# An attention stage on one core: rows of two heads' halves in turn, three strip transfers, masked maxima from a constant, and the subtraction products split over both sets of a step

## The chip, the core and the metric

The kernel runs on one core of a Trainium2 chip. TensorE (PE) multiplies, VectorE (DVE) and ScalarE (ACT) read its results out of PSUM, GpSimd (POOL) works on SBUF alone, and SyncE (SP) issues most transfers. The metric is device time in microseconds (us) of one execution, as the median of several runs; lower is better.

## The reference, cut to what matters

The model is four layers on `x` of 4 batches x 1024 positions x 256 channels: latent attention, a gated feed-forward scan, a delta-rule layer, and the feed-forward scan again. The change lies in the attention alone, whose core is

```python
c_kv = x @ W_dkv.T
q = (x @ W_dq.T @ W_uq.T).reshape(B, T, nh, hs)
q_lat = einsum('bqhd,hdl->bhql', q, k_eff)
attn = einsum('bhql,bkl->bhqk', q_lat, c_kv) / sqrt(hs)   # 16 heads of 16
attn = where(causal, attn, -inf)
attn = softmax(attn, axis=-1)
y = einsum('bhql,hld->bqhd', attn @ c_kv, v_eff)
```

The softmax needs, for every query, its greatest unmasked score before the exponentials are taken.

## The kernel before

The 64 (batch, head) pairs are worked in 16 **units** of four heads (`units`, L77). For each unit three buffers of 128 partitions x 1024 positions hold its strips: `kh` and `kl` (the keys as a high part and a rest) and `q`. Head j of the unit has partitions 32j to 32j+31; in them the 16 key rows stand twice, and beside them in `q` the queries' high part (first 16 rows) and rest (second 16). One product over 32 rows with `kh` and one with `kl` thus give a score of full precision, and the four heads' products lie on four different strips of 32 rows of TensorE's array.

`quad(i, s)` (L366) is one **step**: ten steps make a unit (`STEPS`, L54), and each step does one piece of up to 512 columns for all four heads of *two* units at once:

- for unit i+1 (`first`, in the code `one` is True) the scores with queries on partitions, in two passes (`kh`, `kl`), from which VectorE takes **maxima** (`finish`, L421 to L432). Steps 0 to 2 and 7 to 9 hold the diagonal and use a fused add-mask-and-maximum (L424); steps 3 to 6 are a plain maximum (L430) into `m0`. The diagonal pieces of the second half of the queries start their maximum from that `m0` column.
- for unit i (`second`) the scores with keys on partitions, in three passes: `kh`, `kl`, and `gr` with the weights `minus`, which subtracts each query's greatest score. ScalarE takes the exponentials (L419) into `p`. On diagonal steps a matmul of `identb` with `mb` puts the mask into the bank first (`masks`, L386).

Each of these eight results of a step has a PSUM bank of its own out of a pool of seven (`pss`, L74), which also serves every other small product. A step is issued as two **sets** with the value products of two steps ago between them (L445 to L461; `values`, L480): in the first set the heads 2 and 3 of unit i and 0 and 1 of unit i+1, in the second set the others. All four `gr` products of unit i stand in the first set, on all four strips, so the banks of unit i's heads 0 and 1 are opened there: six banks in the first set, two in the second.

`greatest(i, half)` (L464) turns the 128 x 16 maxima of a half by TensorE into `ps_m`, splits them into a high part and a rest (ACT L470, DVE L471), and sends them through DRAM (`md`) into the `gr` rows. The first half of unit i+1 is turned behind step 4 of `quad(i)`, the second half of unit i behind step 0 of `quad(i)`, straight after that step's second set (L587, put first among the step's places).

`feature` (L272) makes the rows of `kall` and `qall` of one batch (two row blocks `mc`, two column halves `n`) and writes them to DRAM; `heads(i, j)` (L313) fetches unit i's strips from there, six transfers of 16 rows for each head, 24 to a unit, all from SP's queue, which keeps its order. For unit 0 the strips are made directly (`first_feature`, L296).

The order on every engine is written out by hand (`manual_schedule`, L520): the loop from L556 calls `quad`, `values`, and the extra work that was put into `places` of each step. Before unit 0's exponentials comes `quad(-1)`, ten steps with unit 0's maxima alone; the other work of batch 0 (features, `vals`, strips of unit 1) is dealt out over its steps 3 to 9 (L570), the strips of unit 1 behind all features.

## Time and profile before

| | |
|---|---|
| median of 3 runs | 1326.14 us (1324.3 to 1327.25) |
| the profiled execution's own time | 1326.79 us |
| its span (first to last instruction) | 1325.1 us |
| mean granted TensorE clock | 0.98 |
| attention stage | from 0 to about 650 us of the span |
| `quad(-1)` | about 20 to 52 us |
| steps with maxima and exponentials together | about 52 to 622 us, 150 of them |

Engine times are busy times. A busy PE isn't a PE at its peak: its rows overlap, and a row's end is modelled, so the place where a stage begins and the next one begins is the better measure. "PEld" is the loading of weights. In the timeline view a row is start, duration, engine, line, operation, result and operands, shape and count, and in brackets the idle time before it with what ended it. The waits view has who waited for whom, then the total, the number of waits and the longest. `ps_s<-q,kh` with 32 rows is a product for the exponentials or the maxima: the compiler's names put the moving operand first, so `q,kh` is unit i's (exponentials) and `kh,q` unit i+1's (maxima).

### The profile page before, as it was taken

Reading aid. Unit: us, or ns where it says so; the run is one execution under the profiler, and the core shown is the slowest. Engines: PE = TensorE matmul, PEld = TensorE weight load, DVE = VectorE, ACT = ScalarE, POOL = GpSimd, SP = SyncE. Lnnn points to the kernel's source line nnn. Section 1 sums busy time; section 2 is a strip of 40 time slices with the busy share of each in tenths; the row PEclk is TensorE's granted clock in tenths of the full one; section 3 lists DMA queues with packets and bytes.
Section 4 is the critical chain, followed back from the end, with each engine's and each line's share of the span. In section 5 each row is a group of like instructions: output and inputs, shape, how many; then the busy total and the mean of one; then the engine's idle time right before and its main releaser. Section 6 shows DMA issues by size and latency. Waiting matters only on the chain. (4 is left out here: it accounts for less than half of the span.)

```text
span 1325.1 us, 36572 instructions
## 1 busy us (share of the span) xinstructions
PE 1247.8 (94%) x14596; PEld 776.4 (59%) x14596; DVE 840.2 (63%) x2440; ACT 697.5 (53%) x1626; POOL 423.3 (32%) x681
## 2 busy tenths in 40 slices
PE   7899899999999999999999999898988999899997
PEld 3454455545555555555444766665655677677886
DVE  6786678787787877886122454468879767533333
ACT  3266566666666666666623456445655544334432
POOL 1040002323033110122100245346888745535220
PEclk9799899999999999999999999999999999999999
DMA  3812621334221422220300223215364532333210
GB/s 96 208 51 70 186 67 48 79 96 146 68 53 41 133 79 59 67 51 4 112 17 0 78 75 90 80 26 166 99 169 112 139 90 75 111 102 85 64 64 32
DMA packets 118649, 112.23 MB, mean 85 GB/s; under 512 B 46672, under 2 KB 103504, under 8 KB 118480
## 3 DMA queue, kind: packets, MB, share of 16 engines
q1 hardware_dynamic: 95200, 100.39, 27.6%
q10 hardware_dynamic: 23280, 9.51, 2.7%
q8 instruction: 115, 1.88, 0.6%
q14 instruction: 54, 0.44, 0.1%
HBM read 65.22 MB, written 44.63 MB: 83 GB/s over the span
## 5 line engine op out<-in xcount | busy, mean ns | idle before, releaser
L419 ACT ACTIVATE p<-ps_s 128x512 f32<-128x512 f32 (+1 forms) x640 | 319.3, 554 | 199.7 <-PE ps_s L410 196.5
L410 PE MATMUL ps_s<-kh,q 32*128 32x512 f32 (+3 forms) x768 | 189.3, 425 | 8.8 <-DMA q<-qall 5.1
L430 DVE TENSOR_REDUCE m<-ps_s 128x1 f32<-128x512 f32 x256 | 163.0, 681 | 34.9 <-PE ps_s L410 34.5
L410 PE MATMUL ps_s<-q,kh 32*128 32x512 f32 (+3 forms) x768 | 163.2, 424 | 0.4
L488 PE MATMUL ps_y<-p,vb 128*32 128x512 f32 (+3 forms) x1536 | 158.3, 500 | 1.1 <-ACT ys L494 1.0
L410 PE MATMUL ps_s<-kl,q 32*128 32x512 f32 (+3 forms) x768 | 151.7, 357 | 0.0
L424 DVE CUSTOM_DVE_ANT_0 junk<-ps_s,mask,m 128x512 bf16<-128x512 f32 (+3 forms) x256 | 126.4, 545 | 38.3 <-PE ps_s L410 37.6
L424 DVE CUSTOM_DVE_ANT_0 junk<-ps_s,mask 128x512 bf16<-128x512 f32 (+3 forms) x256 | 112.3, 486 | 48.9 <-PE ps_s L410 48.5
L410 PE MATMUL ps_s<-q,kl 32*128 32x512 f32 (+3 forms) x768 | 131.2, 359 | 0.0
L410 PEld LDWEIGHTS ps_s<-q,kh 32*128 32x128 f32 x768 | 73.9, 184 | 77.1 <-issue 45.8
L512 POOL TENSOR_TENSOR xa<-xa,yt 128x256 f32<-128x256 f32 x32 | 23.4, 731 | 275.7 <-DVE yt L508 275.7
L410 PEld LDWEIGHTS ps_s<-kh,q 32*128 32x128 f32 x768 | 89.1, 185 | 28.1 <-ACT p L419 9.8
L410 PE MATMUL ps_s<-gr,minus 32*128 32x512 f32 (+3 forms) x768 | 98.2, 365 | 6.1 <-DMA gr<-md 4.9
L391 PEld LDWEIGHTS <-identb 128*128 128x128 bf16 x512 | 34.4, 98 | 88.2 <-issue 85.8
L410 PEld LDWEIGHTS ps_s<-kl,q 32*128 32x128 f32 x768 | 81.4, 188 | 0.0
L205 POOL TENSOR_SCALAR rs<-mv 128x2 f32<-128x2 f32 x24 | 5.5, 230 | 236.6 <-DVE mv L204 236.6
L410 PEld LDWEIGHTS ps_s<-gr,minus 32*128 32x128 f32 x768 | 67.6, 187 | 19.7 <-DMA gr<-md 5.3
L1120 DVE SCALAR_TENSOR_TENSOR gate<-gate 128x256 f32<-128x256 f32 (+1 forms) x56 | 29.4, 524 | 76.3 <-ACT gate L1099 76.1
L1080 PE MATMUL ps_gate<-xnT,ffn_wi 128*128 128x256 f32 (+1 forms) x224 | 66.0, 418 | 3.5 <-DVE hh L1193 3.3
L1198 POOL TENSOR_TENSOR x<-x,hh 128x256 f32<-128x256 f32 x56 | 44.0, 800 | 75.0 <-ACT hh L1197 54.2
L772 PE MATMUL ps_kqv<-wa,h 128*128 128x512 f32 x128 | 65.5, 634 | 2.4 <-ACT h L762 2.3
L410 PEld LDWEIGHTS ps_s<-q,kl 32*128 32x128 f32 x768 | 67.2, 186 | 0.0
(228 smaller groups left out, 2626.5 us busy)
## 6 DMA issues: line engine op xcount, KB each, us to landing
x<-x SPq DMA_DIRECT2D x30, 512.0 KB
kh<-kall SPq DMA_DIRECT2D x120, 64.0 KB
kl<-kall SPq DMA_DIRECT2D x120, 64.0 KB
q<-qall SPq DMA_DIRECT2D x120, 64.0 KB
kall<-hl SPq DMA_DIRECT2D x14, 512.0 KB
qall<-hl SPq DMA_DIRECT2D x12, 512.0 KB
kept<-gs ACTq DMA_DIRECT2D x32, 192.0 KB
gl<-kept SPq DMA_DIRECT2D x32, 192.0 KB
```

Of the source, the lines that this page charges most:

```text
L205: nc.gpsimd.tensor_scalar(rs, mv[:, :, 1], EPS, None, ALU.add)
L391: nc.tensor.matmul(ps[:, ds(at, P)], identb, mb, start=x == 0 and (False, j) not in begun, stop=True, skip_group_check=True,)
L410: nc.tensor.matmul(ps[:, ds(at, n)], a, m, start=x == 0 and (one, j) not in begun, stop=last, skip_group_check=True,)
L419: nc.scalar.activation(p[:, j, :width], ps[:, :width], AF.Exp)
L424: nc.vector.tensor_tensor_reduce(out=junk[:, :n], in0=ps[:, ds(at, n)], in1=mask[:, 512 - n :], scale=1.0, scalar=-3e38 if qt < 4 else fir ...
L430: nc.vector.tensor_reduce(first.m0[:, j, qt - 4 : qt - 3], ps[:, ds(at, n)], AX.X, ALU.max)
L488: nc.tensor.matmul(u.y[ds(32 * j, 32), q0:], vb[u.b % 2][:, kt, ds((4 * u.g + j) * VS, 32)], u.p[s][:, j, ds(at, n)], start=kt == 0, stop= ...
L512: nc.gpsimd.tensor_tensor(xs, xs, yt.rearrange("p n j d -> p n (j d)"), ALU.add)
L772: nc.tensor.matmul(dst, hT(c, kc), wt[:, kc, :], start=kc == 0, stop=kc == KC - 1)
L1080: nc.tensor.matmul(ps, f["w" + "fic"[j]][:, kc, ds(m * P, P)], k.xnT[:, kc, t, ds(at, width)], start=kc == 0, stop=t == 0 and kc == KC - 1,)
L1120: nc.vector.scalar_tensor_tensor(acts[1], acts[1], 1.0, acts[2], ALU.add, ALU.mult)
L1198: nc.gpsimd.tensor_tensor(x[:, b, :], x[:, b, :], h, ALU.add)
```

## The change

Four edits, in the diff's order.

1. **Rows in turn.** The 32 rows of a head stand as row 0 high, row 0 rest, row 1 high, ... in place of 16 high and then 16 rest. `wk0`, `wq0` and the column that picks the rest (`second_half`, now `odd`, one sum over every other column of the identity) follow it.
2. **Three transfers.** `heads(i, x)` fetches `kh`, `kl` and `q` of a unit by one transfer each of 128 rows, the key rows read twice by a broadcast. For unit 1 the order in `quad(-1)` is laid out anew: the first row block's features in steps 2 and 3, unit 1's strips at step 4 ahead of the other features, which go to steps 4 to 7, `vals` in steps 7 to 9.
3. **Maxima from a constant.** Every fused maximum starts at -3e38. In its place `greatest(i, 1)` begins with one VectorE maximum of `m` and `m0`, 128 x 16, ahead of the turn.
4. **Each set with its own `gr` products.** Both sets run three passes, the third with two products in place of four and none. Each set opens four banks.

```diff
-            nc.gpsimd.memset(second_half, 1.0)
...
+            nc.vector.tensor_reduce(odd, k.ident[:, ds(1, P // 2, step=2)], AX.X, ALU.add)
...
-            rs = ds(64 * u.g + HS * j, HS)
-            k_, q_ = bt.kall.bitcast(F32), bt.qall.bitcast(F32)
-            for a in range(2):
-                to = ds(32 * j + HS * a, HS)
-                for dst, src in ((u.kh, k_[0, rs]), (u.kl, k_[1, rs]), (u.q, q_[a, rs])):
-                    nc.sync.dma_start(out=dst.bitcast(F32)[to, :], in_=src)
+            rs = ds(64 * u.g, 64)
+            if x < 2:
+                dst, src = (u.kh, u.kl)[x], bt.kall.bitcast(F32)[x, rs].unsqueeze(1).broadcast_to([64, 2, T])
+            else:
+                dst, src = u.q, bt.qall.bitcast(F32)[:, rs].rearrange("a r t -> r a t")
+            nc.sync.dma_start(out=dst.bitcast(F32), in_=src)
...
-                            scalar=-3e38 if qt < 4 else first.m0[:, j, qt - 4 : qt - 3],
+                            scalar=-3e38,
...
-                masks((2, 3))
-                for turn_ in range(2):
-                    for one, j in ((False, 2), (True, 0), (False, 3), (True, 1)):
-                        product(one, j, turn_, one and turn_ == 1)
-                for j in (2, 3):
-                    product(False, j, 2, True)
-                for j in (0, 1):
-                    product(False, j, 2, False)
...
+                    masks([j for one, j in order if not one])
+                    for turn_ in range(3):
+                        for one, j in order:
+                            if not (one and turn_ == 2):
+                                product(one, j, turn_, turn_ == (1 if one else 2))
+                    for one, j in order:
+                        finish(one, j)
...
             u = units[i]
+            if half:
+                nc.vector.tensor_tensor(u.m[:, 1], u.m[:, 1], u.m0, ALU.max)
             ps = pss.tile([16, P], F32, tag="s", name="ps_m")
             nc.tensor.transpose(ps, u.m[:, half].rearrange("p j q -> p (j q)"), k.ident)
...
+                        first[2 + n if mc == 0 else 4 + 2 * n + y].append(
+                            lambda mc=mc, n=n, name=name, wt=wt, of=of: feature(0, mc, n, name, wt, of, True)
+                        )
+            for y in range(3):
+                first[4].insert(y, lambda y=y: heads(1, y))
```

More of the change, by code (lines that the diff above doesn't have):

```diff
@@ L123, in attention @@
         minus = wp.tile([P, P], F32R, name="minus")
-        second_half = wp.tile([P, 1], F32, name="second_half")
+        odd = wp.tile([P, 1], F32, name="odd")
         wk0, wq0 = (wp.tile([P, P], F32, name=n) for n in ("wk0", "wq0"))
@@ L133, in first_rows @@
             )
-            for j in range(4):
-                d = second_half[ds(32 * j, 32), :]
-                nc.gpsimd.affine_select(
-                    out=d, in_=d, compare_op=ALU.is_ge, fill=0.0, base=-HS, pattern=[[0, 1]],
-                    channel_multiplier=1,
-                )
             for g in gr:
                 nc.vector.memset(g.bitcast(F32), 0.0)
+            nc.vector.tensor_reduce(odd, k.ident[:, ds(1, P // 2, step=2)], AX.X, ALU.add)
         VS = HS + 1
@@ L173, in attention @@
             nc.scalar.activation(
-                wq0.rearrange("p (j a r) -> p j a r", j=4, a=2)[:, :, a],
+                wq0.rearrange("p (j r a) -> p j r a", j=4, a=2)[:, :, :, a],
                 ps[:, 0, 0:64].rearrange("p (j r) -> p j r", j=4), AF.Copy, scale=-1.0 / math.sqrt(HS),
@@ L184, in attention @@
             nc.scalar.copy(
-                wk0.rearrange("p (j a r) -> p j a r", j=4, a=2)[:, :, a],
+                wk0.rearrange("p (j r a) -> p j r a", j=4, a=2)[:, :, :, a],
                 ps[:, 0:64].rearrange("p (j r) -> p j r", j=4),
@@ L309, in first_feature, with heads @@
                 nc.vector.scalar_tensor_tensor(
-                    u.q[:, cols], hi.bitcast(F32), second_half, ps, ALU.mult, ALU.subtract
+                    u.q[:, cols], hi.bitcast(F32), odd, ps, ALU.mult, ALU.subtract
                 )
-        def heads(i, j):
-            if j == 0:
+        def heads(i, x):
+            if x == 0:
                 name_buffers(i)
@@ L444, in quad @@
             else:
-                masks((2, 3))
-                for turn_ in range(2):
-                    for one, j in ((False, 2), (True, 0), (False, 3), (True, 1)):
-                        product(one, j, turn_, one and turn_ == 1)
-                for j in (2, 3):
-                    product(False, j, 2, True)
-                for j in (0, 1):
-                    product(False, j, 2, False)
-                for one, j in ((False, 2), (True, 0), (False, 3), (True, 1)):
-                    finish(one, j)
-                yield
-                masks((0, 1))
-                for turn_ in range(2):
-                    for one, j in ((False, 0), (True, 2), (False, 1), (True, 3)):
-                        product(one, j, turn_, turn_ == 1)
-                for one, j in ((False, 0), (True, 2), (False, 1), (True, 3)):
-                    finish(one, j)
+                for x, order in enumerate(
+                    (((False, 2), (True, 0), (False, 3), (True, 1)), ((False, 0), (True, 2), (False, 1), (True, 3)))
+                ):
+                    if x == 1:
+                        yield
+                    masks([j for one, j in order if not one])
[5 more added lines that the diff above has]
+                        finish(one, j)
             yield
@@ L542, in attention @@
             del rest[:2]
+            first = [[] for _ in range(NS)]
             for mc in range(KC):
                 for n in range(2):
-                    for name, wt, of in (("kall", wk, "ckv"), ("qall", wq, "qd")):
-                        rest.append(
-                            lambda mc=mc, n=n, name=name, wt=wt, of=of: feature(
-                                0, mc, n, name, wt, of, name == "qall" or n == 1
-                            )
-                        )
-            rest += [lambda j=j: vals(0, j) for j in range(0, NT, 2)]
-            rest[-2:-2] = [lambda j=j: heads(1, j) for j in range(4)]
-            rest.append(lambda: load(2))
+                    for y, (name, wt, of) in enumerate((("kall", wk, "ckv"), ("qall", wq, "qd"))):
+                        first[2 + n if mc == 0 else 4 + 2 * n + y].append(
+                            lambda mc=mc, n=n, name=name, wt=wt, of=of: feature(0, mc, n, name, wt, of, True)
+                        )
+            for y in range(3):
+                first[4].insert(y, lambda y=y: heads(1, y))
+            for j in range(0, NT, 2):
+                first[NS - 3 + (j + 2) // 4].append(lambda j=j: vals(0, j))
+            first[NS - 1].append(lambda: load(2))
             late = []
@@ L567, in attention @@
                 if i < 0:
-                    places[0] += rest[:2]
-                    places[1] += rest[2:4]
-                    for a, f in enumerate(rest[4:]):
-                        places[3 + a * (NS - 3) // len(rest[4:])].append(f)
+                    first[0] += rest[:2]
+                    first[1] += rest[2:4]
+                    places = first
                     rest = []
@@ L581, in attention @@
                 if 0 <= i < NU - 2:
-                    for j in range(4):
-                        places[2 + j].append(lambda i=i, j=j: heads(i + 2, j))
+                    for y in range(3):
+                        places[2 + y].append(lambda i=i, y=y: heads(i + 2, y))
                 if i >= 0:
```

## The prediction

> **What bounds the kernel now.** I read the page's busy shares first (PE 94% of the span, DVE 63%), then busy times by stretches, the waits, and TensorE's timeline step by step. The attention stage ends at about 650 us; after it nothing is edited, so only 0 to 650 us counts. In the stretches (columns: span, then busy time of PE, PEld, DVE, ACT, POOL, granted clock, DMA share, GB/s):

> ```profile
> 52.40:57.80 5.40, 2.86 (x14) 1.46 (x12) 0.98 (x7) 0.79 (x2) 0.00 (x0) 0.50 1.08 121
> 57.80:63.60 5.80, 3.23 (x13) 1.36 (x13) 1.09 (x5) 1.29 (x3) 0.00 (x0) 0.50 1.07 187
> 148.00:160.00 12.00, 7.08 (x50) 2.95 (x50) 4.30 (x14) 3.42 (x7) 0.72 (x1) 0.72 0.59 148
> 160.00:602.00 442.00, 438.51 (x4743) 231.40 (x4735) 346.15 (x1127) 284.44 (x582) 88.11 (x106) 1.00 0.29 76
> ```

> From 160 us TensorE is hardly ever idle while VectorE has 78%; so time is won or lost in TensorE's own queue. Two places wait for transfers, 52 to 64 us and 148 to 155 us. Inside the steps, the price of a pass comes from three passes without a wait (timeline, PE):

> ```profile
> 640.90 0.51 PE L410 MATMUL ps_s<-q,kh 32*128 32x512 f32 x4
> 641.24 0.41 PE L410 MATMUL ps_s<-q,kl 32*128 32x512 f32 x4
> 641.47 0.40 PE L410 MATMUL ps_s<-gr,minus 32*128 32x512 f32 x4
> 641.80 1.07 PE L488 MATMUL ps_y<-p,vb 128*32 128x512 f32 x8
> ```

> Starts are 0.34, 0.23 and 0.33 us apart: 0.90 for three passes of 512 columns; second sets (two passes) take 0.67. So the third pass costs 0.23 (0.18 at 384 columns: 0.73 against 0.55; 0.23 with two pieces: 0.85 against 0.62). And here is a step boundary (372.20 is step 0's second set; `ps_m` turns the maxima; 373.19 is step 1's first set):

> ```profile
> 372.20 0.50 PE L410 MATMUL ps_s<-q,kh 32*128 32x512 f32 x1
> ...
> 372.54 0.39 PE L410 MATMUL ps_s<-q,kl 32*128 32x512 f32 x1
> ...
> 372.87 0.28 PE L468 MATMUL ps_m<-ident,m 128*16 128x128 f32 x1
> ...
> 373.01 0.69 DVE L424 CUSTOM_DVE_ANT_0 junk<-ps_s,mask 128x512 bf16<-128x512 f32 x1 [0.54 <-PE ps_s L410]
> 373.19 0.44 PE L410 MATMUL ps_s<-q,kh 32*128 32x384 f32 x1
> 373.62 0.44 PE L410 MATMUL ps_s<-kh,q 32*128 32x384 f32 x1
> ...
> 374.23 0.08 DVE L424 DVE_READ_ACCUMULATOR2_ANT m<- 128x1 f32 x1
> 374.23 0.27 DVE L471 TENSOR_TENSOR mT<-ps_m,mT 16x128 fp32r<-16x128 f32 x1
> ...
> 374.74 0.75 PE L488 MATMUL ps_y<-p,vb 128*32 128x256 f32 x12
> ```

> `ps_m` starts 0.67 after the set, without a wait. The next first set takes 373.19 to 374.74 = 1.55 in place of 0.73: it opens six banks of seven, and they come free only as ACT and DVE read them. VectorE's last maximum of step 0 is done at 374.31, 1.44 behind `ps_m`.

> **The change part by part**

> *The maximum of `m` and `m0` (edit 3): a new wait.* In the changed kernel's instruction order this VectorE operation stands behind all four fused maxima of step 0, and `ps_m` waits for it, directly behind the second set in TensorE's queue. So `ps_m` moves from the set's end to: last maximum done, 1.44 behind the old end, which is 1.21 behind the new end (the third pass, 0.23); plus the operation, nearest rows 0.15 (128x2, L361) and 0.27 (L471), I take 0.20, plus 0.05 to be seen: TensorE idles **1.45 us**. Behind `ps_m` are queued the mask products and the whole next step, or features and latents; nothing of it can be had earlier. Row: at 373.19 to 373.62 unit i's second product had its bank from the mask, and still stood behind the blocked `kh,q`. Did products overtake one another, this term would be 0; the row says that they don't.

> It happens once per unit; unit 15 has no maxima beside it, unit 0 is in the start below, so 14 times. What it gives back is the next first set's own wait, since every bank is free by then. Seven units (3, 4, 7, 8, 12, 13, 14) have nothing between `ps_m` and step 1, which takes 1.54: 1.45 + 0.23 - 0.81 = 0.87 each, 6.1. Three have latents there (first set 0.73, nothing to give back): 1.68 each, 5.0. Three have features (0.82 or near): 1.6 each, 4.8. One has a turned norm (1.32): 1.1. Sum **+17.0**.

> *Third pass in the second set (edit 4), other steps.* From 70.5 to 622 us I tallied 127 other first sets: 152.5 us, against 110.3 if each took its least, so 42.2 us of waits. Added third passes: 83 x 0.23 + 15 x 0.18 + 29 x 0.23 = 28.5. The first set's third pass, with two products, is taken at full price, since both run at once. What of the waits goes? `gr` products on banks of heads 0 and 1 no longer wait there. A first product that waits for a maximum gains the 0.23 by which the second set is longer. One that waits for head 0's exponential gains nothing, since that now starts a pass later. Set by set (start of the third product + 0.90, or of the fourth, moved 0.23 forward but not before the third, + 0.67, whichever is later) the 127 become 3.2 us longer: **+3.2**. With no forward move +7.0, with both moved -9.0; bounds: no wait goes +28.5, all go -13.7.

> The trace has no pass of two strips alone. [...]

> *Fused maxima without `m0`:* 687 against 747 ns at 512 columns, 60 ns x 16 per unit on VectorE, which is off the path except where a bank waits for it: between 0 and -13, I take **-2**.

> *Three transfers and the new start.* In 52.4 to 63.6 us TensorE waits for unit 1's strips: 24 transfers that SP issues from 45.3 to 58.6. Two sets take 5.38 and 5.27 at half clock; step 1's 1.26 and 1.25 there, scaled by 512/384, make 1.7 each, so 7.2 us are waits. After the change the strips stand behind four features only: VectorE's rows (maxima 2.4 us a step, 0.6 a feature from 30.4) put those at 35, landed by 38. The 1.5 MB come by 44 to 51 at 240 to 121 GB/s (this stretch's rows and 46 to 52 us), needed at 52: in time. From the 7.2 go 0.35 (third pass at half clock) and about 1.2 for unit 0's own wait for the maximum; `quad(-1)`, where VectorE is never idle from 28 to 52.6, gains 16 x 0.06 = 1.0. Sum 6.7, **-7** with a little earlier full clock; bounds 0 and -10. Five small POOL instructions less (2.3 to 3.6 us) lie ahead of data landing at 4.2: nothing. The new sum over the identity is done before that too. Later units' strips are needed a unit ahead: nothing, though SP is relieved of 21 issues of 0.42 us a unit.

> *148 to 155 us:* unit 2's `gr` rows sit in SP's queue behind the feed-forward weights (issued 139.6 to 148.3), 5.3 us of wait. That stays, but the new wait behind step 0 overlaps it: **-1.4**.

> Sum: 17.0 + 3.2 - 2 - 7 - 1.4 = **+9.8**. The profiled execution took 1326.8 for a span of 1325.1, 0.7 above the runs' median; 1326.14 + 9.8 = **1336**.

> **The rivals**

> *A, faster: the first sets' waits go whole.* Four open banks of seven may be few enough that no first product waits; then -13.7 stands for +3.2, the sum is -7, **1319**. For it: the waits view of 160 to 602 us books these waits before products to the readers of the banks (total, times, longest):

> ```profile
> PEld ps_s L410 <- ACT p L419: 14.8, 53, 0.6
> PEld ps_s L410 <- DVE m L424: 3.3, 15, 0.4
> PEld ps_s L410 <- DVE m L430: 3.2, 11, 0.8
> ```

> Against: the third and fourth products already wait for the *previous* step's banks, which edit 4 doesn't free sooner. It decides when less than 4.5 us of the 42 remain.

> *B, much slower: no wait goes.* If the banks stay late by as much as the set grew, +28.5 in place of +3.2 and no -2: **1363**. Against: a late maximum can't be later for a longer set.

> *C, the start isn't regained.* 512 KB transfers might not come faster than 64 KB ones, or `gr` of unit 0 be late behind them: 9.8 + 7 = **1343**.

> *D, the change doesn't do what it adds: the wait is covered.* If VectorE were through with step 0 earlier, half the 17 us would go: **1327**, no difference.

> **How the numbers follow.** Forecast 55% (1329 to 1343), A 17%, B 10%, C 10%, D 8%. The range, 1319 to 1347, reaches to A's time and past C's, and leaves B and the lower half of A out. Faster by over 0.2% (2.7 us, about what a measurement can tell here) is A, 0.17; within it D and an edge of the forecast, 0.09; slower 0.74.

> **What would show it.** Right: `ps_m` behind step 0 with 1.3 to 1.6 us of idle before it, put down to VectorE, and step 1's first set behind it at 0.73; second sets at 0.90; no wait for strips near 52 us; third passes in first sets still 0.23. Wrong: `ps_m` without idle time; first sets at 0.90 throughout (A) or still at 1.2 to 1.5 with second sets at 0.90 (B); fused maxima that keep 747 ns.

## The result

| | median (lowest to highest, runs) | ratio to before, 95% interval |
|---|---|---|
| before | 1326.7 us (1324.3 to 1329.36, 4) | |
| changed | 1334.88 us (1334.3 to 1335.18, 4) | 1.006 [1.0044, 1.0076] |

The kernel became 8.2 us slower (5.8 to 10.1 by the interval); the forecast was +9.8 and 1336. The profiled execution took 1334.74 us with a span of 1332.9 (before: 1325.1).

**The step boundary after.** This is the timeline of the changed kernel at the same place as the one of before, unit 8's step 0 and the start of its step 1 (the step's second set starts at 374.96):

```profile
376.96 0.08 DVE L418 DVE_READ_ACCUMULATOR2_ANT m<- 128x1 f32 x1
376.96 0.17 DVE L457 TENSOR_TENSOR m<-m,m 128x16 f32<-128x16 f32 x1
377.24 0.09 PEld L459 LDWEIGHTS ps_m<-ident,m 128*16 128x16 f32 x1 [1.75 <-ACT p L413]
377.27 0.27 PE L459 MATMUL ps_m<-ident,m 128*16 128x128 f32 x1 [1.35 <-DVE m L457]
...
377.59 0.44 PE L404 MATMUL ps_s<-q,kh 32*128 32x384 f32 x1
377.59 0.44 PE L404 MATMUL ps_s<-kh,q 32*128 32x384 f32 x1
...
378.31 0.86 PE L479 MATMUL ps_y<-p,vb 128*32 128x256 f32 x16
```

VectorE's new operation on `m` starts as soon as the last fused maximum is out, and `ps_m` follows it by 0.31 us. From the second set's start to `ps_m` it is 2.31 (before 0.67): 0.90 for three passes and 1.41 idle (the row's bracket says 1.35, as it counts from the modelled end of the last product; idle times below are by starts, like the 1.41). Behind it the next first set takes 377.59 to 378.31 = 0.72 (before 1.55), its four first products all at once: every bank is free. In all 14 units (1 to 14) `ps_m` waits like this, 1.34 to 1.36 us by the brackets. Note how one wait is booked twice: TensorE's own row names `m`, the row of its weight load names ScalarE's `p`, which was done at 377.04, ahead of the operation on `m` (377.13). The waits view of the changed kernel, 160 to 602 us (total, times, longest), has both bookings of it (first and second row here the weight loads', third TensorE's):

```profile
PEld ps_s L404 <- DVE m L424: 25.3, 56, 0.8
PEld ps_m L459 <- ACT p L413: 20.5, 14, 1.8
PE ps_m L459 <- DVE m L457: 14.9, 11, 1.4
```

The first row is a trap: it looks as if the sets now waited more for maxima (L424 is the plain maximum here). But these weight loads waited while the products before them ran: outside the 14.9 us of the third row, TensorE is idle for only 442.00 - 423.39 - 14.9 = 3.7 us here. By the starts in TensorE's timeline, the sets of 160 to 602 us that value products follow (before's first sets and most of the changed kernel's) stood 41 us above their least times (0.90, 0.73, 0.85 for three passes) in before and 16 in the changed kernel, the first set behind `ps_m` left out; with all other sets it is 43 and 20.

**Busy time by stretches**, changed kernel (span, then PE, PEld, DVE, ACT, POOL, granted clock, DMA share, GB/s):

```profile
51.50:55.00 3.50, 3.37 (x28) 2.07 (x28) 3.50 (x20) 1.67 (x3) 0.00 (x0) 1.00 1.01 303
148.00:160.00 12.00, 10.63 (x85) 4.62 (x77) 7.40 (x19) 6.16 (x12) 0.72 (x1) 0.86 0.51 178
160.00:602.00 442.00, 423.39 (x4576) 218.25 (x4574) 329.37 (x1098) 275.73 (x562) 83.82 (x101) 1.00 0.22 75
```

At 51.5 us TensorE works while the strips come in at 303 GB/s; before it waited there at 121 GB/s. In 148 to 160 it is busy for 10.63 in place of 7.08. In the steady stretch it lost 438.51 - 423.39 = 15.1 us of busy time: the new wait.

**Where the time went.** How much later than in before each unit's step 0 stands (start of its second set, us):

| unit | 1 | 2 | 3 | 6 | 8 | 10 | 12 | 14 | end of attention |
|---|---|---|---|---|---|---|---|---|---|
| changed | -4.6 | -1.7 | -3.6 | -0.2 | +2.8 | +6.7 | +8.4 | +10.0 | +10.3 |

The start gains, then nearly every unit gives some back (from unit 2 to 3 the wait of 148 us gains again). The attention ends 10.3 us later, the span only 7.8: the later stages, which nobody edited, were 2.5 us shorter in this execution.

### The profile page after: what moved, and what is told of

Read it like the earlier page. It is cut to its first block, busy times and chain, and to the rows that moved or that the text cites. A ratio compares the mean times of both kernels' runs of the same rounds, so it can differ in the third digit from the quotient of the medians.

```text
span 1332.9 us, 36102 instructions
## 1 busy us (share of the span) xinstructions
PE 1248.5 (94%) x14596; PEld 770.2 (58%) x14596; DVE 833.6 (63%) x2457; ACT 697.4 (52%) x1626; POOL 421.8 (32%) x676
## 5 line engine op out<-in xcount | busy, mean ns | idle before, releaser
L418 DVE CUSTOM_DVE_ANT_0 junk<-ps_s,mask 128x128 bf16<-128x128 f32 (+3 forms) x512 | 225.9, 487 | 90.6 <-PE ps_s L404 87.5
L404 PE MATMUL ps_s<-kh,q 32*128 32x512 f32 (+3 forms) x768 | 192.2, 428 | 4.8 <-DVE m L424 1.6
L424 DVE TENSOR_REDUCE m<-ps_s 128x1 f32<-128x512 f32 x256 | 163.7, 682 | 26.7 <-PE ps_s L404 26.6
L404 PE MATMUL ps_s<-q,kh 32*128 32x512 f32 (+3 forms) x768 | 156.0, 425 | 0.0
L404 PE MATMUL ps_s<-gr,minus 32*128 32x512 f32 (+3 forms) x768 | 123.6, 345 | 1.3 <-DMA gr<-md 1.3
L404 PEld LDWEIGHTS ps_s<-q,kh 32*128 32x128 f32 x768 | 70.3, 185 | 76.4 <-DVE m L424 27.7
L404 PEld LDWEIGHTS ps_s<-kh,q 32*128 32x128 f32 x768 | 87.6, 186 | 29.6 <-DVE m L418 14.2
L763 PE MATMUL ps_kqv<-wa,h 128*128 128x512 f32 x128 | 68.3, 657 | 2.4 <-ACT h L753 2.3
L1071 PE MATMUL ps_gate<-xnT,ffn_wc 128*128 128x256 f32 (+1 forms) x224 | 65.9, 417 | 1.1 <-ACT gate L1090 0.6
```

The costliest lines, as they stand in the source:

```text
L404: nc.tensor.matmul(ps[:, ds(at, n)], a, m, start=x == 0 and (one, j) not in begun, stop=last, skip_group_check=True,)
L418: nc.vector.tensor_tensor_reduce(out=junk[:, :n], in0=ps[:, ds(at, n)], in1=mask[:, 512 - n :], scale=1.0, scalar=-3e38, op0=ALU.add, op1= ...
L424: nc.vector.tensor_reduce(first.m0[:, j, qt - 4 : qt - 3], ps[:, ds(at, n)], AX.X, ALU.max)
L763: nc.tensor.matmul(dst, hT(c, kc), wt[:, kc, :], start=kc == 0, stop=kc == KC - 1)
L1071: nc.tensor.matmul(ps, f["w" + "fic"[j]][:, kc, ds(m * P, P)], k.xnT[:, kc, t, ds(at, width)], start=kc == 0, stop=t == 0 and kc == KC - 1,)
```

## The experiments

My theory: the late maximum of `m` and `m0` costs about 17 us as an idle stretch of TensorE per unit, the transfers and the start give back 7 to 8, and the sets with their own products are nearly neutral. Rivals: the sets themselves cost the time (B), or save it (A) while something else costs more. Ratios are to runs of before on the same chip, which had a median of 1325.82 (`e1` to `e4`), 1327.35 (`e5` to `e8`) and 1328.27 (`e9`, `e10`). All the kernels compute the whole reference.

**Run e1_max_early.** The changed kernel with the maximum put behind step 9's fused maxima, a whole step ahead of its use:

```diff
+            def early_max():
+                if first is not None and s == NS - 1:
+                    nc.vector.tensor_tensor(first.m[:, 1], first.m[:, 1], first.m0, ALU.max)
...
-            if half:
-                nc.vector.tensor_tensor(u.m[:, 1], u.m[:, 1], u.m0, ALU.max)
```

> The changed kernel with one move: the maximum of m and m0 is issued behind the fused maxima of step 9, so a whole step before the turn that needs it. Wait theory (the forecast's): the 1.4 us of idle TensorE behind step 0's second set go in 14 units, 20 us; in the seven units where step 1 follows at once, its first set waits for banks again, some 0.35 us each, 2.5 us back: 17 us less than the changed kernel's 1334.9, so 1316 to 1320, faster than the kernel before. Pass theory (rival: the loss is the third pass in the second sets, and the wait only stands where waits for banks would): 1333 to 1336, and first sets of step 1 back at 1.5 us.

**Run e2_m0_pointer.** The changed kernel without that operation; the fused maxima start at `m0` again:

```diff
-                            scalar=-3e38,
+                            scalar=-3e38 if qt < 4 else first.m0[:, j, qt - 4 : qt - 3],
...
-            if half:
-                nc.vector.tensor_tensor(u.m[:, 1], u.m[:, 1], u.m0, ALU.max)
```

> The changed kernel with the constant undone: fused maxima start at the m0 column again, and there is no separate maximum. Wait theory: like the early maximum, but with fused maxima of 747 ns for 687 at 512 columns, which costs 0 to 3 us: 1317 to 1323. Pass theory: 1333 to 1338.

Measured: `e1` 1319.05 us, ratio 0.995 [0.9925, 0.9974]; `e2` 1316.76, 0.9927 [0.9904, 0.995]. Without the wait both are faster than before; against the changed kernel's 1.006 they stand 1.1% and 1.3%, or 15 and 18 us, lower. In `e1` the boundary has no wait (timeline of TensorE, unit 8; the second set's third pass, `ps_m`, the next first set):

```profile
370.52 0.40 PE L404 MATMUL ps_s<-gr,minus 32*128 32x512 f32 x2
370.85 0.28 PE L463 MATMUL ps_m<-ident,m 128*16 128x128 f32 x1
...
371.17 0.44 PE L404 MATMUL ps_s<-q,kh 32*128 32x384 f32 x1
371.48 0.44 PE L404 MATMUL ps_s<-kh,q 32*128 32x384 f32 x1
```

`ps_m` starts 0.33 behind the last pass, and the next set's second product waits for its bank 0.31 us, so part of the old wait for banks is back. From unit 1's `ps_m` to unit 15 `e1` goes from 2.9 to 3.7 us ahead of before and `e2` from 6.9 to 6.1: the constant's shorter maxima are worth 1.6 us in these executions. That `e2`'s attention ends earlier all the same comes from the start, where `e1`'s profiled execution ran at half clock for 20.4 us in the first 72, `e2`'s for 6.8. The two medians are 2.3 us apart, which lies within their intervals.

**Run e3_old_sets.** The changed kernel with the sets of before (six banks and two); the late maximum stays:

```diff
-                for x, order in enumerate(
...
+                masks((2, 3))
+                for turn_ in range(2):
+                    for one, j in ((False, 2), (True, 0), (False, 3), (True, 1)):
+                        product(one, j, turn_, one and turn_ == 1)
...
```

> The changed kernel with the sets undone: all four subtraction products in the first set, two passes in the second; the late maximum stays. Wait theory: the third passes (28.5 us) go and the first sets' waits for banks (25 us) come back; the wait behind step 0 ends at the same time behind the second set's start, so it lasts 0.23 us longer: 1329 to 1334. Pass theory: 28 us less than the changed kernel, 1305 to 1309.

Measured: 1343.04 us, 1.0118 [1.009, 1.0147]. This missed: I expected the old sets to be as good or better, and they are 8 us worse. The wait is longer there, 2.34 - 0.67 = 1.67 us, as two passes end earlier; and the granted clock fell to half inside the steps, which I had not reckoned with. `e6` to `e10` follow that up.

**Run e4_strips_start.** Before with the rows in turn, the three transfers and the new start alone (edits 1 and 2). Against the changed kernel it has `e2`'s and `e3`'s edits together:

```diff
-                            scalar=-3e38,
+                            scalar=-3e38 if qt < 4 else first.m0[:, j, qt - 4 : qt - 3],
...
-                for x, order in enumerate(
...
+                masks((2, 3))
...
-                nc.vector.tensor_tensor(u.m[:, 1], u.m[:, 1], u.m0, ALU.max)
```

> The kernel before with the rows in turn, the three transfers and the new order of the start alone. Wait theory: 7 us less than before, 1317 to 1323, all of it ahead of 65 us of the span. Rival (the start isn't regained, or the larger transfers hold up the greatest scores): 1325 to 1328.

Measured: 1315.24 us, 0.9918 [0.9893, 0.9944], a gain of 10.6 (7.4 to 14.2). In its timeline unit 1 is 6.7 us earlier than in before, unit 3 8.4, and from there to the end of attention 8.0 to 8.4: all of the attention's gain lies ahead of 185 us, where the waits for strips and for unit 2's `gr` were. The time is below the 1317 to 1323 that I expected, and not all of the gain lies ahead of 65 us: 1.7 us came at unit 2's `gr`, and 2 of the profiled execution's 10.5 lie behind the attention, where nothing was edited.

**Run e5_sets_alone.** Before with the new sets alone (edit 4):

```diff
-                masks((2, 3))
...
+                    for turn_ in range(3):
+                        for one, j in order:
+                            if not (one and turn_ == 2):
+                                product(one, j, turn_, turn_ == (1 if one else 2))
```

> The kernel before with the sets alone: three passes in both, everything else as before. Forecast's term (third passes +28.5, first sets' waits -25): 1327 to 1331, so no more than 5 us from before. Rival A (the waits go whole): 1311 to 1314. Rival B (no wait goes): 1352 to 1356.

Measured: 1326.78 us, 0.9997 [0.9981, 1.0013]: no difference, with A (1312) and B (1354) far outside. Attention ends 1.9 us later than in before, in the profiled executions. `e2` is `e4` with the new sets, and stands 1.5 us above it.

**Run e6_max_alone.** Before with the constant and the late maximum alone (edit 3):

```diff
-                            scalar=-3e38 if qt < 4 else first.m0[:, j, qt - 4 : qt - 3],
+                            scalar=-3e38,
...
+            if half:
+                nc.vector.tensor_tensor(u.m[:, 1], u.m[:, 1], u.m0, ALU.max)
```

> The kernel before with the constant and the late maximum alone. Behind a second set of two passes the wait lasts 1.65 us in place of 1.4. Idle theory (only the idle time counts, 14 times, less what the next first set waits less, 2 us for faster fused maxima, and 1.4 at unit 2): 1337 to 1341. Clock theory (an idle time of 1.65 us in so many units also lets the granted clock fall to half for 3.4 us, which the old sets with the late maximum showed in several units): 1343 to 1350, with half-clock stretches behind several of the waits.

Measured: 1343.91 us, 1.0148 [1.01, 1.0195]. Edit 3 alone costs 16.6 us by the medians (19.6 by the ratio), more than the idle time explains by my numbers (1337 to 1341), and about what it does with half-clock stretches added (1343 to 1350).

**Run e7_old_sets_max_early.** The transfers and start, the constant, and the maximum behind step 9, with the old sets: the best version by my reading so far. It is `e1` with this edit:

```diff
-                for x, order in enumerate(
...
+                masks((2, 3))
...
```

> The kernel before with the three transfers, the new start, the constant, and the maximum issued behind step 9; old sets. Nothing waits that did not wait before, and fused maxima are 60 ns shorter: 0 to 3 us less than the strips and the start alone (1315.2): 1312 to 1316. If the constant gives nothing: 1315 to 1317. If the operation itself costs, wherever it stands: over 1318.

Measured: 1316.97 us, 0.9926 [0.9903, 0.995]: 10.4 us faster than before, the same as `e4` (10.6). In the timeline its attention ends 12.1 us earlier than in before, `e4`'s 8.4; the medians don't show the difference, and the time is where I expected it for a constant that gives nothing.

**Run e8_longer_wait.** The changed kernel with the maximum computed three times, to lengthen the wait alone:

```diff
             if half:
                 nc.vector.tensor_tensor(u.m[:, 1], u.m[:, 1], u.m0, ALU.max)
+                for _ in range(2):
+                    nc.vector.tensor_tensor(u.m[:, 1], u.m[:, 1], u.m0, ALU.max)
```

> The changed kernel with the maximum of m and m0 taken three times in place of once, one behind the other, which leaves its result as it is: the wait behind step 0 grows by two short VectorE operations, some 0.2 to 0.35 us, to 1.6 to 1.75. Idle theory: 14 x 0.2 to 0.35 more, 3 to 5 us, 1338 to 1340. Clock theory: the same plus half-clock stretches of 3.4 us behind several of the waits, each costing some 1.7 us: 1343 to 1352, and the granted clock in the steps below 1.0 in several units, where the changed kernel has it in one.

Measured: 1351.32 us, 1.0189 [1.0149, 1.0229]. The wait grew from 1.41 to 1.83 us, more than the 1.6 to 1.75 that I expected; 14 x 0.42 makes 5.9 us, and the median grew by 16. In the profiled execution, the fastest of the four (1346.12), attention ends 11.3 us later than in the changed kernel: the 5.9, and three more half-clock stretches at about 1.7 us each. Here is TensorE behind unit 7's wait, first in `e3` at full clock, then in `e8`:

```profile
342.13 0.27 PE L464 MATMUL ps_m<-ident,m 128*16 128x128 f32 x1 [1.60 <-DVE m L462]
...
342.44 0.44 PE L404 MATMUL ps_s<-q,kh 32*128 32x384 f32 x1
...
342.72 0.33 PE L404 MATMUL ps_s<-q,kl 32*128 32x384 f32 x1
...
342.90 0.34 PE L404 MATMUL ps_s<-gr,minus 32*128 32x384 f32 x4
```

```profile
347.50 0.27 PE L461 MATMUL ps_m<-ident,m 128*16 128x128 f32 x1 [1.78 <-DVE m L459]
...
347.81 0.63 PE L404 MATMUL ps_s<-q,kh 32*128 32x384 f32 x1
...
348.24 0.52 PE L404 MATMUL ps_s<-q,kl 32*128 32x384 f32 x1
...
348.56 0.53 PE L404 MATMUL ps_s<-gr,minus 32*128 32x384 f32 x2
```

The same passes start 0.43 and 0.32 apart in place of 0.28 and 0.18, and a product takes 0.63 in place of 0.44. The granted clock is 0.5 from 347.9 on, for 3.4 us.

**Run e10_filled_wait.** `e8` with TensorE kept busy during the wait, with the same operations on VectorE's path:

```diff
+            for _ in range(7 if half else 0):
+                nc.tensor.matmul(ps, k.ident[:, :16], k.ident, start=True, stop=True)
             nc.tensor.transpose(ps, u.m[:, half].rearrange("p j q -> p (j q)"), k.ident)
```

> The kernel with the maximum computed three times, whose wait of 1.83 us per unit was followed in some units by a half-clock stretch of 3.4 us, and in it TensorE is kept busy in the wait: seven products of the identity with its own first 16 columns (128 columns each) stand ahead of the turn and are overwritten by it. The path through VectorE is the same length. If the half-clock stretches come from TensorE's idle time, they go between 160 and 620 us (without the products: 347.9, 385.4, 614.1), and the time falls to 1338 to 1346 with a granted clock of 1.00 throughout these units, although no path is shorter. If they come from elsewhere (the strips, the moment in the run), three to six of them stay, and the time stays at 1346 to 1355. If the seven products take longer than the wait, the units grow by that and the time rises above 1355.

Measured: 1339.31 us, 1.0081 [1.0054, 1.0108]: 12 us less than `e8` (by the ratios 14, and the intervals don't meet) with more work. The products fill 1.70 us of the wait, and no half-clock stretch is left in the profiled execution from 160 us to the last unit. The granted clock is the third column from the right; here behind unit 7's wait in `e8` (`ps_m` at 347.50), then in `e10` around and behind it (346.3):

```profile
347.00:352.00 5.00, 4.50 (x45) 2.65 (x45) 1.96 (x8) 1.88 (x5) 0.00 (x0) 0.66 0.03 7
```

```profile
343.50:347.00 3.50, 3.45 (x37) 2.40 (x38) 2.20 (x10) 1.69 (x4) 0.00 (x0) 1.00 0.00 0
347.00:350.50 3.50, 3.50 (x66) 2.21 (x62) 2.63 (x12) 2.34 (x6) 0.00 (x0) 1.00 0.04 12
```

So in these runs it is TensorE's idle time that brings the stretches on, not the late maximum as such: three from 160 us on in `e8`, none where 1.70 of the 1.83 us are filled. `e3` has 20.5 and `e6` 17.1 us of them from 160 us on, about 10 and 8 us lost, which is of the size of what these two lost beyond the idle time. Not all of the 12 us is seen in a trace: between the two profiled executions attention ends 4.5 us earlier in `e10`, 1.3 of it since `ps_m` starts 2.64 behind the set in place of 2.73. The executions without a trace have their mean granted clock on record: `e8`'s four go from 0.982 at 1346.12 us down to 0.971 at 1357.3, `e10`'s seven lie between 0.985 and 0.992. The two kernels ran on different chips; their ratios are to before on the same one.

**Run e9_weights_later.** `e7` with one more edit that neither kernel has, to be rid of the wait at 148 us:

```diff
-                if i == 1:
-                    k.load_ffn()
...
+                    if i == 2 and s == 5:
+                        k.load_ffn()
```

> The strips, rows and start of the change, the maxima from the constant with their operation behind step 9 (no wait behind step 0), the sets of before, and one more edit that neither kernel has: the feed-forward weights are requested behind step 5 of unit 2 in place of the end of unit 1, so that unit 2's rows of greatest scores are not queued behind them. If the wait of 148 to 155 us is those weights, some 5 us of idle time and a half-clock stretch (3.4 us of it in the runs without late maximum, worth about 1.7) go on top of the 10.4 that the same kernel without this edit gained: 1309 to 1312 against 1327, and the stretch 148 to 160 us shows a granted clock of 1.00. If the rows are late for another reason, it stays at 1316 to 1318.

Measured: 1305.36 us (1303.41 to 1307.56, 4 runs), 0.9827 [0.9806, 0.9848]: faster than both kernels, 22.9 us less than before, and less than the 1309 to 1312 that I expected. The stretch that had 7.08 us of TensorE before and 10.63 in the changed kernel:

```profile
148.00:160.00 12.00, 11.60 (x106) 5.70 (x106) 8.90 (x19) 7.67 (x16) 0.73 (x1) 1.00 0.66 224
```

From unit 2 to unit 3 it wins 7.1 us on before where `e7` wins 0.5, so the difference is 6.6, as reckoned (5 and 1.7). Against `e7` the medians say 11.6, the profiled executions 7.0 and the ends of attention 5.3; the two ran on different chips, and what the rest is stays open.

## Why the prediction was right

**The new wait (+17.0).** Right in place, mechanism and size. The idle time is 1.41 for 1.45. Net per unit, by the shift of the timeline from the second set of step 0 to the end of step 1's first set, it cost 0.8 in each of the seven units with nothing in between (forecast 0.87), 1.6 behind latents (1.68), 1.3 to 1.5 behind features (1.6), 0.9 in unit 11 (1.1); 15.9 in all for 17.0. Taking the wait away returned 15 (`e1`) and 18 us (`e2`). That TensorE's products don't overtake one another, which carried the term, held in the boundary's rows: behind the wait `ps_m` starts at 377.27, the next set's first products at 377.59. The operation took 0.17 us where I had 0.20; the 0.05 for its end to be seen was my guess and came from no row, and `ps_m` started 0.14 behind that end (377.13).

**The third pass (+3.2).** Right within its bounds: +1.9 at the end of attention in `e5`, +1.5 between `e4` and `e2`, nothing measurable in `e5`'s median (-2.5 to +1.7 us). The added passes are met almost whole by shorter waits: in 160 to 602 us they are 68 x 0.23 + 24 x 0.18 + 24 x 0.23 = 25.5, and the waits fell by 41 - 16 = 25 (43 - 20 = 23 with all sets). A failed because 16 us of waits stayed where it needed less than 4.5, B because the waits do shrink. A third pass with two products is as dear as one with four, as the term took it: sets of three passes at 512 columns that wait for nothing take about 0.90 in both kernels.

**Fused maxima (-2).** In the page's groups (count, then busy time, mean ns), before and then changed:

```profile
L424 DVE CUSTOM_DVE_ANT_0 junk<-ps_s,mask,m 128x512 bf16<-128x512 f32 (+3 forms) x256 | 126.4, 545 | 38.3 <-PE ps_s L410 37.6
L424 DVE CUSTOM_DVE_ANT_0 junk<-ps_s,mask 128x512 bf16<-128x512 f32 (+3 forms) x256 | 112.3, 486 | 48.9 <-PE ps_s L410 48.5
```

```profile
L418 DVE CUSTOM_DVE_ANT_0 junk<-ps_s,mask 128x128 bf16<-128x128 f32 (+3 forms) x512 | 225.9, 487 | 90.6 <-PE ps_s L404 87.5
```

All are at the cheaper price, 13 us less of VectorE. What of it reaches the end is 1.6 us by the timelines of `e1` and `e2` from unit 1 on; no median shows it by itself.

**Start (-7) and 148 us (-1.4).** The mechanism was right, and in the timeline the size too. Behind unit 0's step the changed kernel was 6.8 us ahead, of which 4.6 were left at unit 1: its clock was at half until 70.1 us, before's until 70.3, so the kernel that was further ahead did more of its work at half clock. Between units 2 and 3, where the `gr` wait lies, it won 3.4. `e4` shows both without the late maximum: 6.7 and 1.7 in the timeline, 8.4 together as forecast, but 10.6 in the median. The 2 us by which the median says more lie behind attention in the profiled execution; no run shows why.

**What the sum did not hold.** The sum's size came out since two errors were small and opposite: attention ends +10.3 (forecast +9.8), and the unedited rest of the execution was 2.5 us shorter. The sum had no term for the granted clock inside the steps. In the changed kernel that is one stretch (534.3 us, about 1.7 us), so nothing was noticed, and that is luck and not reckoning; with 0.26 us more of idle time per unit, `e3` had five stretches, one of double length, and lost some 10 us by them. The sets with their own products, which I took for a small cost, are what keeps it there: their third pass makes the wait 1.41 in place of 1.67. That second effect of edit 4 was not in the forecast. So edit 4 is worth nothing alone (`e5`) and 8 us beside edit 3 (1.0118 of `e3` against 1.006, with intervals that don't meet): the terms of this change don't add.

**C and D.** C's condition (no gain at the start) is refuted by `e4`, D's (a covered wait) by the row at 377.27.

## What to carry to other kernels

A cheap operation (0.17 us here) is priced by the place where it stands in the queue of the engine it blocks: put behind the last of a batch and ahead of `ps_m`, where TensorE then started nothing for 1.41 us a unit, it cost some 16 us, where it has a step's time to spare nothing. Take the edits of a change one by one in the reckoning, but then look for pairs that share a wait, since a cost that hides another's idle time has no price of its own. And when a wait for a transfer is found in the profile, look at what stands ahead of it in the issuing queue: moving one unrelated load gave 5 to 12 us.

## What the runs showed of the hardware

**Half clock behind idle times of 1.41 to 1.83 us.** From 160 us to the last unit, the granted clock in the profiled executions fell to 0.5 for 3.4 us (twice 6.8) as follows, each time behind the idle time of a step 0:

| kernel | idle time of TensorE behind step 0 | units followed by half clock |
|---|---|---|
| before, e1, e2, e4, e5, e7, e9 | none | none |
| changed | 1.41 us | 12 |
| e3 | 1.67 us | 5, 7, 8, 12, 14 |
| e6 | 1.67 us | 7, 8, 12, 14 |
| e8 | 1.83 us | 7, 8, 14 (and unit 1) |
| e10 | 1.83 us, 1.70 of it filled | none |

The stretch begins between 0 and 1.5 us behind the idle time (once 0.09 ahead of its end) and costs about half its length: in `e8`, units with nothing between `ps_m` and step 1 fell 0.3 to 1.3 us further behind before without a stretch and 2.2 to 2.8 with one. Which units are hit isn't a matter of their idle time alone, since all 14 have the same. Executions differ too: the ten runs of `e3` go from 1332.71 us at a mean granted clock of 0.988 to 1345.9 us at 0.974.

| kernel | idle time | whole: followed by half clock | split over two intervals: followed |
|---|---|---|---|
| changed | 1.41 us | 1 of 11 | 0 of 3 |
| e3 | 1.67 us | 5 of 9 | 0 of 5 |
| e6 | 1.67 us | 4 of 8 | 0 of 6 |
| e8 | 1.83 us | 4 of 4 | 0 of 10 |

Each of the 14 stretches starts at the very end of the interval that held the wait. So in these executions the place of a wait on the grid counts first (14 of the 32 whole waits were followed by half clock, none of the 24 split ones): `e8`'s wait is longer than `e3`'s, and it is hit less often since only four of its waits lie whole in an interval. The longer a whole wait, the more often it was followed (1 of 11 at 1.41 us, 9 of 17 at 1.67, 4 of 4 at 1.83); what decides among those of 1.41 and 1.67 us stays open.
